# A graph layer on one core: pairs of node tiles, edges by node quarter, operands in PSUM

## The chip, the core and the metric

The kernel runs on one core of one Trainium2 chip. The metric is device time in microseconds (us), lower is better; a kernel's time is the median of several runs. The profile is one execution recorded by the hardware profiler. Engines: PE (TensorE matmul; PEld its weight loads), DVE (VectorE), ACT (ScalarE), POOL (GpSimd), SP (issues plain DMAs). SBUF is the on-chip memory of 128 partitions, PSUM the matmul's output memory of eight banks.

## The reference

One layer over a graph of N = 6250 nodes with D = 256 features and 206,250 edges (`src`, `dst`, sorted by `dst`). Three branches share a normalised input, and a mixture of experts follows:

```python
xn = layernorm(x)
# graph attention, 4 heads of 64
h = xn @ W;  el = h @ Wl.T;  er = h @ Wr.T
e = exp(leaky_relu(el[src] + er[dst], 0.2))
w = e / maximum(segment_sum(e, src), 1e-12)[src]
gnn = elu(stack([segment_sum(w[:, k:k+1] * h[dst], src) for k in range(4)], 1) + b)
# linear attention over all nodes (q softmax over features, k over nodes), rms norms
mix = rmsnorm(linear_attention(rmsnorm(xn)) @ w_out + b_out) + xn
x = x + gnn.reshape(N, 256) + mix
# eight experts of 256 hidden units, each node takes the best two
t = layernorm(x)
out = x + t + sum_e combine[:, e] * (gelu(t @ w1[e] + b1[e]) @ w2[e] + b2[e])
```

So every edge needs the row `h[dst]` with `er[dst]`, and its weighted sum lands at `src`. The edges come sorted by `dst`, so the kernel sorts them by `src` itself.

## The kernel before

Nodes are in 49 tiles of 128 (NT), edges in 1612 columns of 128 (EC, one edge per partition). The work has three parts.

**Sort and projection** (to about 632 us). The loop at the end of the first part calls `project` for 13 groups of four node tiles (layer norm statistics on DVE, transposes and one projection matmul on PE, q, k, v and the rows of the gather table `table`, 64 features and 4 values er), and `sort_batch` for 51 batches of BW = 32 edge columns, three after each group. `sort_batch` builds a one-hot `ob` of each edge's tile number `src >> 7` (50 columns; L320), counts per column (`n_ps` L326), scans them (L330), takes off the count itself (`before` L335), and finds by matmuls (`r_ps` L349, L350) each edge's rank among the batch's edges of its tile. Rank and a one-hot of ranks `ohp` (L372) place the edge's two f16 numbers (`rv` L368, parts of `dst` and of the place in the tile) by matmul into `g_ps` (L377), copied to `grid`: for each tile, each batch and each rank one edge. `context` then computes the attention's 128 x 128 context (key maximum `kmax` L293, `kv` L414). After that the block at L476 to L515 scans the counts of all batches and writes `to_p` and `to_c`, the partition and column at which every edge of a tile will stand.

**Edges** (from 645.5 us on). For each node tile b:

- `pack(b)`: one-hots of column (`ohc` L785) and partition (`ohp` L799) of each edge; `rc` (L791) is `ohc` times the edge's numbers; 51 matmuls into `s_ps` (L804) give the tile's 35 columns of edges (CPT) densely. From it come the row numbers `dst_x` (L813) and the place of the source within the tile, `loc` (L819).
- `gather(dst_x)` (L824, L830): 35 indirect DMAs, one per column, each bringing 128 rows of 68 floats into a seventh of `xe` (pieces of EB = 7 columns, 12 buffers). POOL issues them.
- `sources(b, k, ...)`, five times per tile, called one tile ahead by `look`: `oh` (L842, one-hot of `loc`, 7 x 128), seven transposes `t_ps` (L850), a copy to SBUF `ohT` (L852, ACT), seven matmuls with `elp` into `e_ps` (L854): el of each edge's source.
- `weights`: sum of three parts (L862), five additions of the gathered er (L867), leaky ReLU (L868), exp to `ew` (L870).
- `sums`, five times: the one-hot cast to f32 `oh32` (L875, ACT), `v` = row x weight for the four heads (L879, DVE, two operands in SBUF), seven matmuls `a_ps` (L887) that add 260 columns at the source's place in the tile.
- `heads` divides by the sum of the weights into `x2`.

**Attention and experts** run in pieces between these. `some_more()` is called once after each `sums`, so five times per tile, and performs the next piece of the generators in `todo`: first the 39 pieces of `attention()`, then, appended after each group of four tiles, `finish_steps`: `front` (elu, second layer norm, transposes `tokT` L648, router logits L653), `route` (top two; a matmul for `b2`, L704), eight `expert(e)` (`h_ps` L714, gelu `hT` L722 on ACT, `y_ps` L726, `x` L730 on DVE) and `store`. `h_ps` and `y_ps` have two PSUM buffers each. Groups are of four tiles, the last of one.

The framework's scheduler orders the instructions of each engine from this program and puts the waits in. POOL's queue holds, during the edge part, nothing but the gathers, in order of `pack`. The order of calls around the gathers is:

```python
for k in range(nk):                       # nk = 5
    sums(k, ohs[k], xes[k], ew, a_ps)
    if b + 1 < NT:
        look(b + 1, k)
    if k == 1 and b + 2 < NT:
        dst_x, loc = pack(b + 2)
        ready[b + 2] = (gather(dst_x), loc)
    some_more()
```

A second program follows under `tc.If(over_n > 0)`: if a tile has too many edges for its columns (`flag`), the sums are computed column by column.

Of the kernel before, what the change touches and what calls it, by code (L numbers as in the profile page):

```python
# [8 lines left out]
F32 = mybir.dt.float32  # L9
# [8 lines left out]
P = 128  # L18
GT = 4
BW = 32  # L20
# [3 lines left out]
EB = 7  # L24
# [3 lines left out]
def tile_gps_layer(  # L28
# [40 lines left out]
    NBT = -(-EC // BW)  # L69
    NB = NT + NT % 2  # L70
    BB = 512 // NB
    BB = 8 if BB > 8 else BB
    assert BW % BB == 0 and CPT % EB == 0
    TW = FO + H
    VW = HF + H
    PW = 3 * HID + TW + H
    KW = 2 * HID + 1
    O_TAB = 3 * HID
    O_EL = O_TAB + TW
    assert NPAD > N and PW <= 512 and last > 0  # L80

    groups = [(t0, min(GT, NT - t0)) for t0 in range(0, NT, GT)]

# [9 lines left out]
    nc.vector.tensor_copy(iota_f, iota_i)  # L93
    iota_h = cp.tile([P, P], F16, name="iota_h")
    nc.vector.tensor_copy(iota_h, iota_i)
    iota_b = cp.tile([P, P], BF16, name="iota_b")
    nc.vector.tensor_copy(iota_b, iota_i)
# [11 lines left out]
    elp = cp.tile([P, NT, 3, H], BF16, name="elp")  # L109
# [3 lines left out]
    grid = cp.tile([P, NT, NBT, 2, 2], F16, name="grid")  # L113
# [39 lines left out]
    def load_edges(pool):  # L153
        return load_ids(pool, "src_i", src, NT * P), load_ids(pool, "dst_i", dst, N)
# [19 lines left out]
    tri = sp.tile([P, P], F16, name="tri")  # L174
    nc.vector.tensor_scalar(tri, iota_f, piota, None, op0=OP.is_gt)
    ones16 = sp.tile([P, P], F16, name="ones16")
    nc.vector.memset(ones16, 1.0)
    delta = sp.tile([NB, NB], F16, name="delta")
    nc.vector.tensor_scalar(delta, iota_f[:NB, :NB], piota[:NB], None, op0=OP.is_equal)
    ntot = cp.tile([NT, NBT], F32, name="ntot")  # L180
# [5 lines left out]
    with tc.tile_pool(name="ids", bufs=1) as lp:  # L186
# [4 lines left out]
        def twice(a):  # L191
            return a[:, :, None].to_broadcast([P, EC, 2])

        nc.vector.tensor_single_scalar(t_i, src_i, 7, op=OP.logical_shift_right)
        nc.vector.tensor_copy(bid, twice(t_i))
        nc.vector.tensor_single_scalar(t_i2, dst_i, 3, op=OP.logical_shift_right)
        nc.gpsimd.tensor_copy(va, twice(t_i2))
        nc.vector.tensor_scalar(
            dst_i, dst_i, 7, 8, op0=OP.bitwise_and, op1=OP.logical_shift_left
        )  # L200
        nc.vector.tensor_single_scalar(src_i, src_i, P - 1, op=OP.bitwise_and)
        nc.vector.scalar_tensor_tensor(t_i, src_i, 1.0, dst_i, op0=OP.add, op1=OP.add)
# [5 lines left out]
        out=wcat[:, :, O_TAB:O_TAB + FO], in_=gnn_W.rearrange("(c p) f -> p c f", p=P)  # L208
# [21 lines left out]
    for c in range(DC):  # L230
        wt_ps = mps.tile([FO, P], F32, name="tp")
        nc.tensor.transpose(wt_ps, wcat[:, c, O_TAB:O_TAB + FO], ident)
# [4 lines left out]
        nc.scalar.copy(wcat[:, c, O_TAB + FO:PW], wlr_ps)  # L237
# [9 lines left out]
    def project(t0, n):  # L247
# [16 lines left out]
        tab = qw.tile([P, GT, TW], F32, name="tab")  # L264
        for j in range(n):
            t = t0 + j
            xn = qw.tile([P, D], F32, name="xn")
            nc.vector.tensor_scalar(
                xn, xt[:, j, :], stats[:, t, 0:1], rstd[:, t:t + 1],
                op0=OP.subtract, op1=OP.mult,  # L270
# [15 lines left out]
            nc.scalar.copy(tab[:, j, :], pr[:, O_TAB:O_EL])  # L286
            nc.vector.tensor_copy(el[:, t, :], pr[:, O_EL:PW])
            rows = P if t < NT - 1 else last
            k_t = kv[:rows, t, :HID]
            if t == 0:  # L290
                nc.vector.tensor_copy(kmax, k_t)
            else:
                nc.vector.tensor_max(kmax[:rows], kmax[:rows], k_t)  # L293
        nc.sync.dma_start(
            out=table[t0 * P:(t0 + n) * P, :].rearrange("(t p) f -> p t f", p=P),
            in_=tab[:, :n, :],
# [9 lines left out]
    def sort_batch(t):  # L306
        c0 = t * BW
        w = min(BW, EC - c0)
        cs = slice(c0, c0 + w)

# [13 lines left out]
        n_ps = sps.tile([NB, BW], F32, name="n_ps")  # L324
        for c in range(w):
            nc.tensor.matmul(  # L326
                n_ps[:, c:c + 1], lhsT=ob[:, c, :], rhs=ones16[:, 0:1], start=True, stop=True
            )
        inc = sw.tile([NB, BW], F32, name="inc")
        nc.vector.tensor_tensor_scan(  # L330
            inc[:, :w], ones[:NB, 0:1].to_broadcast([NB, w]), n_ps[:, :w], 0.0,
            op0=OP.mult, op1=OP.add,
        )
        before = sw.tile([NB, BW, 2], F16, name="before")
        nc.vector.tensor_tensor(  # L335
            before[:, :w], inc[:, :w, None].to_broadcast([NB, w, 2]),
            n_ps[:, :w, None].to_broadcast([NB, w, 2]), op=OP.subtract,
        )
        nc.scalar.copy(ntot[:, t:t + 1], inc[:NT, w - 1:w])
        ahead = sw.tile([NB, BW, NB], F16, name="ahead", bufs=1)  # L340
        nc.vector.tensor_tensor(
            pairs(ahead[:, :w]), two(before[:, :w], NB // 2), row(delta, NB // 2), op=OP.mult
# [3 lines left out]
        for i, a in enumerate(range(0, w, BB)):  # L346
            z = min(w, a + BB)
            part = r_ps[:, i, :(z - a) * NB]
            nc.tensor.matmul(part, lhsT=tri, rhs=flat(ob[:, a:z]), start=True, stop=False)  # L349
            nc.tensor.matmul(  # L350
                part, lhsT=ones16[:NB, :], rhs=flat(ahead[:, a:z]), start=False, stop=True
            )
        nf = w // BB
        nc.scalar.copy(
            r16[:, :nf * BB, :].rearrange("p (i c) b -> p i (c b)", c=BB),
            r_ps[:, :nf, :BB * NB],
        )
# [3 lines left out]
        rank = sw.tile([P, BW], F16, name="rank")  # L361
        with nc.allow_low_precision("one summand of each sum is not zero"):
            nc.vector.tensor_reduce(rank[:, :w], r16[:, :w], axis=AX.X, op=OP.add)
        rank2 = sw.tile([P, BW, 2], F16, name="rank2")
        nc.vector.tensor_copy(rank2[:, :w], rank[:, :w, None].to_broadcast([P, w, 2]))
# [9 lines left out]
        g_ps = sps.tile([P, 2 * NB], F32, name="g_ps")  # L375
        for c in range(w):
            nc.tensor.matmul(  # L377
                g_ps, lhsT=ohp[:, c, :], rhs=flat(rv[:, c]), start=(c == 0), stop=(c == w - 1)
            )
# [675 lines left out]
```

## Time and profile before

| | us |
|---|---|
| median of 9 runs | 4252.88 (4215.78 to 4276.84) |
| profiled execution | 4219.04, of which the span is 4217.3 |
| first gather starts | 645.5 |
| last gather starts | 4075.1 |
| gathers | 1715, 947 ns the median of one, 1962.5 in all |
| `a_ps` L887 matmuls on PE | 938.3 in all (3430 passes) |
| `v` L879 on DVE | 493.1 in all (245) |
| `ohp` L799 of 2048 elements on DVE | 177.6 in all (147) |
| POOL idle until `loc` L819 comes | 1463.0 in 20 waits, 624.3 of them the first |

A row of the profile's group list gives an instruction's line, engine, operation, the names of what it writes and reads, shapes and count; then the busy time of all, the mean duration of one, and the idle time just before them with what ended it. "remote" is an end that the profile can put down to no instruction of its list; "issue" is time in which the engine waited for nothing that the profile shows. A matmul in f32 runs in two passes, so L887 counts 3430 for 1715 matmuls. PEclk is the clock that PE was granted, as a share of full speed. In windows, the numbers after a span are busy microseconds of each engine with the count of instructions.

### The profile page before, as it was taken

The page shows a single profiled execution, that of the slowest core. Times are in us where ns is not written, and L with a number is a line of the kernel's source. Part 1 is how long each engine was busy: PE and PEld are TensorE (multiplying, and loading weights), DVE is VectorE, ACT ScalarE, POOL GpSimd, SP SyncE. Part 2 cuts the span into 40 slices and gives each one's busy share as a digit, 9 for nine tenths or more (in the row PEclk, how much of TensorE's full clock was granted, in tenths as well). Part 3 has the DMA queues.
Part 4 walks back from the last instruction along what each step waited for, and adds up shares of the span by engine and source line. Part 5 has one row for each costly group of instructions (what it writes and reads, how often), then busy time and mean ns, then how long its engine had stood idle before and what let it go on. Part 6 is the DMA issues. An engine that isn't in the chain of part 4 may idle for free.

```text
span 4217.3 us, 42641 instructions
## 1 busy us (share of the span) xinstructions
PE 2557.0 (61%) x16398; PEld 1805.8 (43%) x16398; DVE 2078.4 (49%) x3763; ACT 1053.2 (25%) x1888; POOL 1969.3 (47%) x1726
## 2 busy tenths in 40 slices
PE   6888772464467776547457276186275376562758
PEld 3444541343354544425335155154254254452546
DVE  8888993464573443524435145145135245352443
ACT  2323221242332231222222022022122223121223
POOL 0000006676774364643735725725636447557330
PEclk9777765776788877768678688587587688775879
DMA  1000101122131010100101101101101001111010
GB/s 53 19 19 16 9 1 33 40 49 47 40 84 22 13 31 15 29 17 17 29 12 21 31 10 21 32 10 23 25 12 29 17 17 29 18 22 29 12 18 7
DMA packets 106661, 103.22 MB, mean 24 GB/s; under 512 B 42694, under 2 KB 78756, under 8 KB 106452
## 3 DMA queue, kind: packets, MB, share of 16 engines
q0 software_dynamic: 54880, 59.82, 8.3%
q1 hardware_dynamic: 49876, 39.73, 3.1%
q8 instruction: 131, 2.15, 0.2%
q10 hardware_dynamic: 1696, 0.89, 0.1%
q14 instruction: 78, 0.64, 0.1%
HBM read 85.69 MB, written 14.63 MB: 24 GB/s over the span
## 4 chain that ended last, share of the span: by engine, by line
PE 25%; another core or an unknown queue 19%; issue 10%; POOL 9%; DVE 4%; ACT 2%; DMA 1%; DVEq 0%; ACTq 0%; POOLq 0%
POOL xe L830 9%; PE y_ps L726 8%; PE a_ps L887 8%; PE h_ps L714 7%; DVE v L879 2%; PE t_ps L850 1%; PE y_ps L704 1%; ACT ohT L852 1%; DMA xe<-table,dst_x 1%; PE y_ps L653 1%; DVE rc L791 0%; ACT hT L722 0%; DVE ohp L799 0%; PE s_ps L804 0%
## 5 line engine op out<-in xcount | busy, mean ns | idle before, releaser
L830 POOL DMA_INDIRECT xe<-table,dst_x x1715 | 1962.5, 1144 | 2092.4 <-DVE loc L819 1463.0
L887 PE MATMUL a_ps<-v,oh 128*128 128x260 f32 x3430 | 938.3, 425 | 133.3 <-DVE v L879 97.0
L887 PEld LDWEIGHTS a_ps<-v,oh 128*128 128x128 f32 x3430 | 714.8, 214 | 268.3 <-issue 117.3
L879 DVE TENSOR_TENSOR v<-xe,ew 128x1792 f32<-128x1792 f32 x245 | 493.1, 2020 | 523.4 <-remote 285.0
L726 PE MATMUL y_ps<-w2s,hT 128*128 128x256 f32 x1568 | 436.1, 422 | 304.2 <-issue 158.7
L875 ACT CAST oh<-oh 128x896 f32<-128x896 bf16 x245 | 230.0, 939 | 1252.5 <-PE a_ps L887 782.9
L730 DVE SCALAR_TENSOR_TENSOR x<-y_ps,comb,x 128x256 f32<-128x256 f32 x392 | 183.7, 482 | 644.2 <-remote 379.1
L726 PEld LDWEIGHTS y_ps<-w2s,hT 128*128 128x128 f32 x1568 | 307.9, 207 | 433.6 <-issue 213.9
L714 PE MATMUL h_ps<-tokT,w1s 128*128 128x512 f32 (+1 forms) x832 | 392.2, 594 | 2.7 <-ACT hT L722 2.7
L852 ACT COPY ohT<-t_ps 128x896 bf16<-128x896 bf16 x245 | 220.8, 901 | 438.4 <-remote 302.0
L854 PE MATMUL e_ps<-elp,ohT 128*128 128x12 bf16 x1715 | 82.1, 171 | 319.1 <-ACT ohT L852 178.1
L804 PE MATMUL s_ps<-rc,ohp 128*128 128x72 f16 x2499 | 122.8, 210 | 216.6 <-issue 163.0
L854 PEld LDWEIGHTS <-ohT 128*128 128x128 bf16 x1715 | 68.9, 99 | 379.7 <-ACT ohT L852 222.4
L722 ACT ACTIVATE hT<-h_ps,b1s 128x512 f32<-128x512 f32 (+1 forms) x208 | 135.4, 662 | 331.1 <-PE h_ps L714 175.3
L804 PEld LDWEIGHTS <-ohp 128*128 128x128 f16 x2499 | 109.2, 108 | 235.8 <-issue 176.8
L799 DVE TENSOR_TENSOR ohp<-to_p,iota_h 128x2048 f16<-128x2048 f16 x196 | 193.5, 1000 | 28.7 <-remote 17.7
L653 PE MATMUL y_ps<-rwT,tokT 128*128 128x8 f32 x196 | 34.9, 287 | 253.7 <-ACT tokT L649 138.8
L714 PEld LDWEIGHTS h_ps<-tokT,w1s 128*128 128x128 f32 x832 | 145.5, 196 | 98.0 <-issue 91.7
L867 DVE TENSOR_TENSOR z<-z,xe 128x28 f32<-128x28 f32 x245 | 44.0, 186 | 253.6 <-DMA xe<-table,dst_x 214.0
L842 DVE TENSOR_TENSOR oh<-iota_b,loc 128x896 bf16<-128x896 bf16 x245 | 147.9, 617 | 41.1 <-issue 25.4
L377 PE MATMUL g_ps<-rv,ohp 128*128 128x100 f16 x1612 | 111.9, 245 | 82.7 <-DVE ohp L372 82.7
L850 PE MATMUL t_ps<-identb,oh 128*128 128x128 bf16 x1715 | 159.4, 237 | 4.1 <-ACT ohT L852 3.8
(229 smaller groups left out, 2801.5 us busy)
## 6 DMA issues: line engine op xcount, KB each, us to landing
xe<-table,dst_x POOLq DMA_INDIRECT x1715
xt<-in_x_dram SPq DMA_DIRECT2D x24, 512.0 KB
base_y<-xt SPq DMA_DIRECT2D x12, 512.0 KB
yt<-base_y SPq DMA_DIRECT2D x12, 512.0 KB
out_dram<-x SPq DMA_DIRECT2D x12, 512.0 KB
w1s<-in_L_ffn_w_dram SPq DMA_DIRECT2D x8, 256.0 KB
w2s<-in_L_ffn_w_dram SPq DMA_DIRECT2D x8, 256.0 KB
table<-tab SPq DMA_DIRECT2D x12, 136.0 KB
```

The lines of the kernel that those rows point to most:

```text
L714: nc.tensor.matmul(h_ps[:, :w], lhsT=w1s[:, e, c, f * P:(f + 1) * P], rhs=tokT[:, c, :w], start=(c == 0), stop=(c == DC - 1),)
L726: nc.tensor.matmul(y_ps, lhsT=hT[:, f, j * P:(j + 1) * P], rhs=w2s[:, e, f, :], start=(f == 0), stop=(f == FC - 1),)
L730: nc.vector.scalar_tensor_tensor(x2[:, j, :], y_ps, comb[:, j, e:e + 1], x2[:, j, :], op0=OP.mult, op1=OP.add,)
L799: nc.vector.tensor_tensor(pairs(ohp[:, :m]), twos(to_p[:, b, t0:t0 + m], P // 2), iota_2.to_broadcast([P, m, P // 2, 2]), op=OP.is_equal,)
L804: nc.tensor.matmul(flat(s_ps), lhsT=ohp[:, t - t0, :], rhs=flat(rc[:, t]), start=(t == 0), stop=(t == NBT - 1),)
L830: nc.gpsimd.indirect_dma_start(out=xe[:, j, :], out_offset=None, in_=table, in_offset=bass.IndirectOffsetOnAxis(ap=dst_x[:, c:c + 1], axis=0),
L850: nc.tensor.transpose(t_ps[:, j, :], oh[:, j, :], identb)
L852: nc.scalar.copy(ohT, t_ps)
L854: nc.tensor.matmul(e_ps[:, k * EB + j, :], lhsT=ohT[:, j, :], rhs=elp[:, b].rearrange("p i h -> p (i h)"), start=True, stop=True,)
L875: nc.scalar.copy(oh32, oh)
L879: nc.vector.tensor_tensor(v[:, :, :HF].rearrange("p j (h f) -> p j h f", h=H), xe[:, :, None, :FO].to_broadcast([P, EB, H, FO]), e_k[:, :, ...
L887: nc.tensor.matmul(a_ps, lhsT=oh32[:, j, :], rhs=v[:, j, :], start=(c == 0), stop=(c == CPT - 1),)
```

## The change

1. **Pairs of tiles.** The sort's key is `src >> 8`: 25 pairs (NQ), so 26 columns (NB) in place of 50. Ranks and `grid` are per block of CB = 16 edge columns (101 blocks NBT), two blocks to a batch of 32. The count matmul has two columns (one, none), so one scan with resets gives the exclusive counts, negated, and `before` goes; the lower triangle `tri` becomes `upto`. The reduce works on a folded half; the doubled rank is copied by ACT.
2. **Projection.** The normalised input `xn` is computed by ACT, `el` is copied by POOL from the projected rows, the key maximum is one reduce at the end, `kv - krow` is done by POOL. A table row has 69 floats: er, the 64 features, a one.
3. **Placing moves into `pack(q)`,** which now runs per pair, 25 times: one-hots of the edge's node quarter, two matmuls and a scan for each tile of the pair, folds, and the place `to` for the 101 blocks. Then as before `ohc`, `rc`, `ohp`, `s_ps`, with 72 columns instead of 36, in seven chunks of 16 blocks. Two times 35 gathers are issued at once. A tile's edges are in order of the quarter (S = 4, SN = 32 nodes) of their source; with fixed windows of columns, a column can hold edges of one or two neighbouring quarters, 45 cells of column and quarter in all (CELLS).
4. **Operands in PSUM.** One bank holds `ew_s` (a copy of `ew`), the bias `gb_s`, the iotas `iota_p` (f16) and `iota_q` (bf16) and `edges`, the pair's numbers, copied in by `pack`. `hps` drops from two buffers to one.
5. **`look`** (in place of `sources`): one `oh` of 12 x 4 x 32 bf16, 12 transposes, two copies `ohT`, one matmul that clears `e_ps` and 12 with 48 columns (`elw`: for each quarter its own rows of el, zero elsewhere).
6. **`sums`**, four times per tile: `ohw` = one-hot x weight (f32, 10 to 12 columns x 4 heads x 32 nodes), and a matmul for each cell with the gathered rows as weights (65 columns, the ones give the sum of weights) and 128 columns of `ohw`. `v` and the cast of `oh` go. The result is transposed: a copy `a_s` and four transposes bring it back to nodes by features.
7. **Buffers.** `xe` is a whole tile of 35 columns, three buffers; the gathered er is added in one operation, kept in the program's order.
8. **Order.** `pack(q + 1)` is called in the pair's first tile at k = 1. `some_more()` is called four times per tile. `expert` is split into `hidden` and `result`: the first layer of expert e alternates with the second of e - 1. Groups for the experts are 11 of four tiles, then 3, 1 and 1.
9. The overflow flag is computed at the end, from counts kept by `pack`.

The core of the diff:

```diff
-        nc.vector.tensor_single_scalar(t_i, src_i, 7, op=OP.logical_shift_right)
+        nc.vector.tensor_single_scalar(t_i, src_i, 8, op=OP.logical_shift_right)
...
+    def pack(q):
...
+        for u in range(U):
+            ohs = gw.tile([P, S, NBT], F16, name="ohs")
+            nc.vector.tensor_tensor(
+                ohs, uh[:, None, :].to_broadcast([P, S, NBT]), quarter[:, u], op=OP.is_equal
+            )
+            here = pl.tile([P, S, NBT], F32, name="s_ps")
+            nc.tensor.matmul(flat(here), lhsT=upto, rhs=flat(ohs), start=True, stop=True)
+            total = pt.tile([P, S, NBT], F32, name="t_ps")
+            nc.tensor.matmul(flat(total), lhsT=ones16, rhs=flat(ohs), start=True, stop=True)
+            nc.vector.tensor_tensor_scan(
+                flat(inc[:, u]), ones[:, 0:1].to_broadcast([P, S * NBT]), flat(total),
+                float(u * CW * P), op0=OP.mult, op1=OP.add,
+            )
...
+        nc.vector.tensor_copy(
+            edges, grid[:, q].rearrange("p t i two -> p (t i two)").bitcast(F32)
+        )
...
+            ohc = gw.tile([P, PB, U * CW], F16, name="ohc")
+            nc.vector.tensor_tensor(
+                pairs(ohc[:, :m]), twos(to[:, 0, t0:t0 + m], U * CW // 2),
+                iota_2[:, :, :U * CW // 2].to_broadcast([P, m, U * CW // 2, 2]),
+                op=OP.is_equal,
+            )
...
+            ready[q * U + u] = (gather(dst_x[:, u * CW:u * CW + CPT]), loc)
...
-        for k in range(CPT // EB):
-            xe = gw.tile([P, EB, TW], F32, name="xe", bufs=12)
+        xe = gw.tile([P, CPT, TW], F32, name="xe", bufs=3)
+        for c in range(CPT):
+            nc.gpsimd.indirect_dma_start(
...
+        tc.keep_in_program_order(nc.vector.tensor_add(z, z, xe[:, :, :H]))
...
+        nc.vector.tensor_copy(ew_s, ew)
...
+    def sums(i, oh, xe, a_ps):
+        g0, g1 = CELLS[i]
...
+        nc.vector.tensor_tensor(
+            ohw[:, :n],
+            oh[:, g0:g1, i, None, :].to_broadcast([P, n, H, SN]),
+            ew_s[:, c0:c0 + n, :, None].to_broadcast([P, n, H, SN]),
+            op=OP.mult,
+        )
+        for c in range(c0, c0 + n):
+            nc.tensor.matmul(
+                a_ps[:, i].rearrange("f h n -> f (h n)"),
+                lhsT=xe[:, c, H:],
+                rhs=ohw[:, c - c0].rearrange("p h n -> p (h n)"),
+                start=(c == c0), stop=(c == c0 + n - 1),
+            )
...
+                if k == 1 and b % U == 0 and b + U < NT:
+                    pack(b // U + 1)
```

## The prediction

> **What bounds the kernel now.** I read the busy shares and the chain first, then windows stage by stage, then waits and the timeline of one period. The page's rows:
>
> ```profile
> span 4217.3 us, 42641 instructions
> PE 2557.0 (61%) x16398; PEld 1805.8 (43%) x16398; DVE 2078.4 (49%) x3763; ACT 1053.2 (25%) x1888; POOL 1969.3 (47%) x1726
> PE 25%; another core or an unknown queue 19%; issue 10%; POOL 9%; DVE 4%; ACT 2%; DMA 1%; DVEq 0%; ACTq 0%; POOLq 0%
> ```
>
> No engine is busy for more than 61%, and the chain has 19% that it can give to nobody: the stages must be taken apart. Windows (span, then busy time of PE, PEld, DVE, ACT, POOL, PEclk, DMA) of the sort, 0 to 632 us:
>
> ```profile
> 0.00:358.00 358.00, 273.31 (x2263) 151.67 (x2264) 305.85 (x560) 107.70 (x297) 6.86 (x11) 0.80 0.10 29
> 358.00:632.00 274.00, 207.64 (x1801) 128.13 (x1800) 248.22 (x376) 79.89 (x179) 0.00 (x0) 0.71 0.06 7
> ```
>
> DVE works 554 of 632 us (88%) and PE 481 (76%): the sort is bound by DVE, PE close behind. POOL has nothing to do; its first gather starts at 645.5 us. From there the kernel is one loop of 49 node tiles. From 1702.7 to 3473.0 us 24 tiles take 1770.3 us, 73.8 us each, and four tiles make a period: 105 gathers, a pause, 35 gathers, a pause. One period, and the 35 gathers of it cut in two:
>
> ```profile
> 1999.10:2150.90 151.80, 52.78 (x401) 42.81 (x400) 50.42 (x80) 25.00 (x38) 120.04 (x105) 0.65 0.15 28
> 2150.90:2216.60 65.70, 59.61 (x302) 40.77 (x303) 38.10 (x84) 23.79 (x38) 0.01 (x1) 0.90 0.01 1
> 2216.60:2263.80 47.20, 27.55 (x115) 18.55 (x114) 11.13 (x18) 6.45 (x9) 36.84 (x35) 0.81 0.13 25
> 2263.80:2290.40 26.60, 24.86 (x180) 19.41 (x179) 17.18 (x30) 10.12 (x16) 0.03 (x1) 0.95 0.10 22
> ```
>
> ```profile
> 2216.60:2237.60 21.00, 20.33 (x100) 13.97 (x98) 10.16 (x16) 5.77 (x8) 17.02 (x14) 1.00 0.12 23
> 2237.60:2263.80 26.20, 7.22 (x17) 4.58 (x16) 0.97 (x2) 0.69 (x1) 19.81 (x21) 0.66 0.14 27
> ```
>
> While no gather runs, PE is busy 84.5 of 92.3 us (over all six periods 0.90); while gathers run, 80.3 of 199. A burst begins well (PE 97% of 21 us), then everything but POOL nearly stops (PE 28%, in three like windows 15 to 34%, mean of the four 0.24). The timeline shows the stop:
>
> ```profile
> 1791.95 0.94 ACT L875 CAST oh<-oh 128x896 f32<-128x896 bf16 x1 [18.22 <-remote]
> 1792.02 2.03 DVE L879 TENSOR_TENSOR v<-xe,ew 128x1792 f32<-128x1792 f32 x1 [17.74 <-remote]
> 1792.30 2.57 POOL L830 DMA_INDIRECT xe<-table,dst_x  x1 [0.30 <-DMA xe<-table,dst_x]
> ...
> 1795.17 0.95 POOL L830 DMA_INDIRECT xe<-table,dst_x  x1 [0.30 <-issue]
> ...
> 1860.74 0.37 ACT L649 COPY tokT<-y_ps 128x256 f32<-128x256 f32 x1 [34.08 <-remote]
> ```
>
> ACT and DVE wait 18 and 34 us for something from PE, which is idle too; the last wait ends 6 us after the burst's last gather. So hand-offs from PE come late while gathers follow one another cleanly. Why, the trace doesn't tell. The loop is bound by gather time plus PE work that doesn't fit beside it. Third line: a gather that meets a v (L879) takes 2.57 us in place of 0.95; 152 of 1715 do, 248.7 us more in all. A clean gather is 0.95 us plus 0.30 of issue, 1.25 us, 43.75 us per tile.
>
> **The sort.** Buckets fall from 50 to 26 columns. Prices from the same operations at two sizes: f16 tensor_tensor 966 ns at 1600, 2281 at 4096 elements, so 123 + 0.527 per element, 0.56 us at 832; the reduce 1800 ns at 1600 and 768 at 600, so 0.61 us at 448. Per batch: five operations (ob, ahead, r, two rv) 5 x (0.97 - 0.56) = -2.03; reduce -1.19, fold +0.34 (384 elements); `before` -0.20; rank copy -0.18; a scan twice as long at most +0.2, taken +0.1. Sum -3.16, x 51 = -161 us. In project and context: xn -19.5 (to ACT, busy 188 of the 632 us), running kmax -13.4, its one reduce of 6144 elements +6.3, kv minus krow -8.3 (to idle POOL, ahead of its first gather), el copies -8 (same queue), shift 13 x 0.2 = +2.6: -40. DVE 554 to 353 us. PE: rank matmuls halve, -83 of 166.4 us (L349, L350), 481 to 398; PE is the bound now. At the share that the binding engine has today (0.88) 398 / 0.88 = 453 us. The placing stage goes (13 us after 632 stay for pack, in which DVE is busy 13.3); pack of a pair has 34,744 elements x 0.59 = 20.5 us and some 25 small ones at 0.2 to 0.5, 30 to 37 us. First gather at 490, not 645.5: **-155** us. Bounds: PE at 0.80, 398 / 0.80 + 35 = 533 (-112); DVE at 0.88, 353 / 0.88 + 35 = 438 (-207).
>
> **PE in the loop, per tile.** Before: 164.8 / 4 = 41.2 us. a_ps now 70 passes x 0.274 = 19.1; then 45 matmuls of two passes with 128 columns: 90 x 0.159 (h_ps 128x128, 10.2 us by 64) = 14.3, or 90 x 0.208 (its weight loads today) = 18.7; taken 16, -3.1. Transposes 35 to 12, -2.1; e_ps 35 to 13, -0.9; s_ps 50 of 144 columns at 0.075 (g_ps of 100: 0.069), +1.3; here and total 2 x 0.42 (r_ps rows of 400), +0.8; four head transposes 4 x 0.26 (L648), +1.0. Sum 38.2 us.
>
> **DVE and ACT in the loop.** v (5 x 2.02 = 10.1 us) goes; ohw has 5760 elements, 6.5 us at v's 1.13 ns. Pack: 12,036 elements to 17,372 per tile, +3.2; scans, folds, copies of pack +4 (some 20 operations per pair, 0.2 to 0.5 us); one oh of 1536 for five of 896, -2.2; the five z additions become one, -0.7; the rest +3. 29.2 to 33 us, under PE. ACT loses the oh32 cast (4.7 us) and half of ohT (2.5): it waits 782.9 us for a_ps today, so that earns nothing by itself.
>
> These DVE prices hold if an operand in PSUM costs nothing. No row has a 16-bit tensor_tensor with one. Lower bound 0.59 ns per element (L799, 1217 ns by 2048), upper 1.13 (v, f32): 18,900 x 0.54 = +10.2 us per tile. I take the lower: operand width is what the rows differ by. Trainium skill, "VectorE: DVE Perf Modes", "The perf-mode tier table": a tensor_tensor with any operand in PSUM runs at 1x, half the 16-bit rate; the section "Why PSUM operands drop a tier" bars only a mode that tensor_tensor never has. By the table DVE has 10.2 us more per tile, and the sum would be 4288 in place of 3785 if all of that set the end.
>
> What the move buys shows in the 2.57 us row: with ew_s, iotas and edges in PSUM, a large DVE operation has one SBUF input, and gathers should all take 1.25 us. Against the gain: the 41.8 us after 1702.7, full of v and ohp, have PE at 81% beside slow gathers, while the clean stretch after it has 17%. Cleaner gathers may also mean a longer stop.
>
> **The order of gathers.** Pack now runs once per pair and issues 70 gathers in a row. In the program's DVE order the first tile's z addition comes only 27 to 46 instructions after dst_x and waits for the whole tile (43.75 us); behind it on DVE are the next ohw and the expert sums, which PE waits for. Today this wait is 214 us in 31 times (L867). Whatever is late there is the first tile of a pair; its second is hidden beside the first's work. So per pair: 87.5 us of gathers; in it PE does 0.97 x 21 = 20.4 us, then 66.5 us at 0.20 (between 0.24 above and 0.17 in the long clean stretch) = 13.3; the other 76.4 - 33.7 = 42.7 us at 0.90 take 47.5 us. 135 us per pair, 67.5 per tile, 6.3 less than 73.8. For 40 tiles 252 us; the first nine, beside attention (59 us per tile today, 332 gathers in 560 us), get half, 28. **-280**, bounds 0 (the stop begins after 10 us: 9.7 + 77.5 x 0.17 = 22.9, rest 59.5, 147 per pair) and -530 (0.35 in the stop, 124 per pair, counted in the same way).
>
> **The tail.** After the last gather 141 us pass, PE busy 119. The last blocks are 3, 1 and 1 tiles in place of 4 and 1, so a block less is left, but one-tile experts load the same weights: **-30**, bounds -60 and +10.
>
> **Sum.** Profiled execution: 4219.0 (span 4217.3 and 1.7 around it) - 155 - 280 - 30 = 3754. The median of the runs shown, 4252.88, is 1.008 times that; so the median after is 3754 x 1.008 = 3785 us. Timed runs spread by 0.7% either way; about 0.5% is what a comparison can tell from none.
>
> **Rivals**, as medians.
> 1. *Only the sort earns.* Clean bursts of 70 stop PE as long as the two bounds above say: (4219 - 155 - 30) x 1.008 = 4066. For it the 17% stretch; against it fewer and larger hand-offs (12 transposes, two ohT copies). Chance 0.20.
> 2. *The stop goes away.* If it comes from the number of PE's hand-offs, which falls by a quarter, POOL and PE run side by side: 43.75 us of gathers per tile, PE 38.2 / 0.90 = 42.4 beside them, some 5 for the pause at each pack: 490 + 49 x 49 + 110 = 3001, or 3025. For it: the first 21 us of a burst. Against: stops of 35-gather bursts with 17 instructions in them. Chance 0.13; half-way cases lie between.
> 3. *Slower: DVE with operands in PSUM.* Place: ohc, rc, ohp of pack and oh; price 10.2 us per tile. Pack stands ahead of each pair's gathers, POOL waits for it, and DVE at 43 us passes PE's 38. If all of it is on the path, 49 x 10.2 = +500: 3754 + 500 = 4254, or 4288 (+0.8%). It decides from (4219 - 3754) / 49 = 9.5 us per tile, 0.50 ns per element, on. Against it: DVE has 42% idle in the loop. Chance 0.14.
> 4. *The change doesn't do what it says*: a quarter overflows its cells and the slow path runs. That is a loop of 1612 columns, far above all this; 0.01.
>
> **The numbers.** Forecast 3785, chance 0.52, its own range 3600 to 3980 (front and loop half-way to their bounds). Range 3390 to 4250: it leaves out most of rival 2 and the upper part of 3. Faster 0.82 (forecast, 2, and 0.17 of rival 1), within 0.5% 0.04 (0.03 of 1, 0.01 of 3), slower 0.14 (0.13 of 3, and 4).
>
> **What would show it.** First gather at 440 to 530 us. ohp of 2048 elements near 1.2 us (right) or 2.3 (rival 3). Gathers at 0.95 us nearly all, none of 2.6. 70-gather bursts with PE above 0.9 in the first 20 us and about 0.2 later. About 135 us per pair. Wrong if pairs take 147 or under 110, or if the binding engine in the sort is idle for over 20%.

## The result and the profile after

The changed kernel takes 4704.26 us (median of 20 runs, 4688.76 to 4712.37) beside 4237.91 us for the kernel before: ratio 1.113, 95% interval 1.1108 to 1.1151 (the two medians alone give 1.110). Forecast were 3785 us, range 3390 to 4250. One thing must be known to read the rest: the runs fall into groups in which the kernel before takes 4208 to 4238 us (the first, with this result), 3348 to 3352 us (the second), 4071 us (the third) and 3349 us (the last run), and every ratio below is against the kernel before in the same group. The record gives the chips of these groups the numbers 1, 11, 2 and again 1, so it doesn't tell whether what differs is the chip or something that changed on it.

The profiled execution after has a span of 4690.6 us, 473.3 more than before. Three marks cut it:

| part | before | after | difference | predicted |
|---|---|---|---|---|
| start to first gather | 645.5 | 455.1 | -190.4 | -155 |
| first to last gather's end | 3430.6 | 4100.7 | +670.1 | -280 |
| last gather's end to the end | 141.2 | 134.8 | -6.4 | -30 |

The page after, its span, busy times and chain:

```profile
span 4690.6 us, 39432 instructions
PE 2329.6 (50%) x15347; PEld 1675.7 (36%) x15347; DVE 1967.9 (42%) x4111; ACT 715.2 (15%) x1467; POOL 1674.8 (36%) x1779
another core or an unknown queue 41%; PE 23%; DVE 19%; issue 6%; ACT 2%; POOL 1%; DMA 0%; DVEq 0%; ACTq 0%; SPq 0%
```

Every engine has less work than before, and the share of the chain that belongs to nobody has gone from 19% to 41%. Windows after (span, busy time of PE, PEld, DVE, ACT, POOL, PEclk, DMA): the sort in two pieces, then one pair of tiles, its 70 gathers and the pause after them, and the next burst cut in two:

```profile
0.00:300.00 300.00, 238.58 (x2688) 137.64 (x2689) 258.47 (x537) 145.58 (x456) 24.71 (x49) 0.82 0.14 40
300.00:440.00 140.00, 92.70 (x1216) 64.99 (x1216) 128.87 (x229) 44.72 (x124) 23.84 (x15) 0.60 0.11 2
...
2118.10:2205.30 87.20, 23.39 (x102) 16.03 (x99) 9.49 (x15) 1.96 (x3) 66.14 (x70) 0.59 0.15 28
2205.30:2294.80 89.50, 68.19 (x401) 52.46 (x402) 51.93 (x100) 15.56 (x22) 0.05 (x1) 0.81 0.03 7
2294.80:2309.30 14.50, 12.79 (x126) 11.80 (x124) 14.06 (x25) 4.82 (x6) 11.42 (x11) 1.00 0.25 61
2309.30:2383.50 74.20, 5.70 (x25) 4.85 (x24) 1.96 (x5) 0.74 (x2) 56.22 (x60) 0.53 0.16 28
```

This pair takes 177 us; later ones alternate between about 161 and 177, 85 us per tile on the mean, where four tiles took 295 and one 73.8. In the burst that is cut in two PE falls from 88% to 8% after 14.5 us and stays there for 74 us. That burst is a sharp one: over the 24 bursts of 70 gathers PE is busy for 62% of the first 14.5 us and 14% of the rest, 19.1 us of work per burst. The gathers themselves and the largest group beside them, with the waits (engine and line waiting, for what, us in all, times, longest):

```profile
L927 POOL DMA_INDIRECT xe<-table,dst_x x1715 | 1626.3, 948 | 2574.3 <-PE a_ps L996 1740.1
...
L989 DVE TENSOR_TENSOR ohw<-oh,bank 128x1280 f32<-128x1280 bf16 x196 | 323.0, 1648 | 1058.5 <-remote 847.6
```

```profile
DVE ohw L989 <- remote: 847.6, 28, 57.3
ACT ohT L956 <- remote: 817.4, 12, 95.0
```

The mean of a gather is 948 ns where it was 1144, and 1697 of 1715 are under 1 us (1389 before): the change did to the gathers what it says. DVE and ACT wait for PE up to 95 us, against 56 before. The timeline of the burst that begins at 2294.8 us:

```profile
2308.54 0.82 PE L996 MATMUL a_ps<-ohw,xe 128*65 128x128 f32 x6
...
2333.02 0.37 ACT L675 COPY tokT<-y_ps 128x256 f32<-128x256 f32 x1 [27.70 <-remote]
...
2334.78 1.49 PE L996 MATMUL a_ps<-ohw,xe 128*65 128x128 f32 x6
2360.38 0.17 DVE L683 COPY lg<-y_ps 128x8 f32<-128x8 f32 x1 [26.73 <-remote]
```

PE does a piece in a few microseconds and then 24 us pass before ACT or DVE sees it. A hand-off is the semaphore update with which PE tells that a piece is done. Counted over the trace's semaphore records, each put to the PE instruction that ended last before it, PE's hand-offs came late by 5964 us in sum while gathers ran (643 hand-offs, the latest by 75 us) and by 80 us while none ran; before it was 1565 and 83 us. These sums are estimates: the trace has 2609 update records for PE's 2726 hand-offs, and nearly all that are missing belong to gather time. The recorded hand-offs of DVE and ACT in the same time are late by 0.6 us at most, so it is PE's that are held.

### The profile page after: what moved, and what is told of

Same layout as the page of the kernel before. It is cut to its first block, busy times and chain, and to the rows that moved or that the text cites. A ratio compares the mean times of both kernels' runs of the same rounds, so it can differ in the third digit from the quotient of the medians.

```text
span 4690.6 us, 39432 instructions
## 1 busy us (share of the span) xinstructions
PE 2329.6 (50%) x15347; PEld 1675.7 (36%) x15347; DVE 1967.9 (42%) x4111; ACT 715.2 (15%) x1467; POOL 1674.8 (36%) x1779
## 4 chain that ended last, share of the span: by engine, by line
another core or an unknown queue 41%; PE 23%; DVE 19%; issue 6%; ACT 2%; POOL 1%; DMA 0%; DVEq 0%; ACTq 0%; SPq 0%
PE a_ps L996 8%; PE h_ps L739 5%; PE y_ps L755 5%; DVE rc L889 4%; DVE ohp L894 4%; DVE ohc L882 2%; DVE ohw L989 2%; DVE inc L853 1%; PE y_ps L679 1%; DVE x L759 1%; POOL xe L927 1%; PE y_ps L730 1%; PE y_ps L567 1%; ACT ohT L956 0%
## 5 line engine op out<-in xcount | busy, mean ns | idle before, releaser
L927 POOL DMA_INDIRECT xe<-table,dst_x x1715 | 1626.3, 948 | 2574.3 <-PE a_ps L996 1740.1
L996 PE MATMUL a_ps<-ohw,xe 128*65 128x128 f32 x4410 | 671.4, 308 | 475.1 <-issue 433.9
L996 PEld LDWEIGHTS a_ps<-ohw,xe 128*65 128x65 f32 x4410 | 591.7, 160 | 535.0 <-issue 480.8
L989 DVE TENSOR_TENSOR ohw<-oh,bank 128x1280 f32<-128x1280 bf16 x196 | 323.0, 1648 | 1058.5 <-remote 847.6
L739 PE MATMUL h_ps<-tokT,w1s 128*128 128x512 f32 (+2 forms) x896 | 425.2, 596 | 87.0 <-ACT hT L747 69.9
L899 PE MATMUL s_ps<-rc,ohp 128*128 128x144 f16 x2525 | 263.6, 279 | 189.6 <-DVE ohp L894 189.6
L899 PEld LDWEIGHTS <-ohp 128*128 128x128 f16 x2525 | 227.6, 123 | 259.9 <-DVE ohp L894 249.6
L747 ACT ACTIVATE hT<-h_ps,b1s 128x512 f32<-128x512 f32 (+2 forms) x224 | 142.1, 634 | 1112.5 <-PE h_ps L739 365.7
L889 DVE TENSOR_TENSOR rc<-ohc,bank 128x1152 f16<-128x1152 f16 (+1 forms) x350 | 226.5, 686 | 1.4
L894 DVE TENSOR_TENSOR ohp<-to,bank 128x2048 f16<-128x2048 f16 (+1 forms) x175 | 193.6, 1106 | 0.0
L567 PE MATMUL y_ps<-cw,qT 128*128 128x256 f32 x98 | 47.5, 576 | 266.6 <-ACT qT L565 162.0
```

The source lines that it names most:

```text
L567: nc.tensor.matmul(o_ps, lhsT=qT, rhs=cw, start=True, stop=True)
L739: nc.tensor.matmul(h_ps[:, :w], lhsT=w1s[:, e, c, f * P:(f + 1) * P], rhs=held["tokT"][:, c, :w], start=(c == 0), stop=(c == DC - 1),)
L747: nc.scalar.activation(held[e][:, f, :w], h_ps[:, :w], AF.Gelu, bias=b1s[:, k:k + 1])
L889: nc.vector.tensor_tensor(pairs(rc[:, :m, i, :]), pairs(ohc[:, :m]), twos(edges_q[:, t0:t0 + m, i, :], U * CW // 2), op=OP.mult,)
L894: nc.vector.tensor_tensor(pairs(ohp[:, :m]), twos(to[:, 1, t0:t0 + m], P // 2), iota_2.to_broadcast([P, m, P // 2, 2]), op=OP.is_equal,)
L899: nc.tensor.matmul(flat(s_ps), lhsT=ohp[:, t - t0, :], rhs=flat(rc[:, t - t0]), start=(t == 0), stop=(t == NBT - 1),)
```

## The experiments

Each is an edit of the changed kernel unless said otherwise.

**First group (kernel before 4208 to 4236 us).**

The operands back in SBUF:

```diff
-    bank = pv.tile([P, 512], F32, name="bank")
+    bank = gw.tile([P, 512], F32, name="bank", bufs=1)
```

> The changed kernel with the bank of operands (weights, bias, iotas, the pair's edge numbers) in SBUF instead of PSUM, nothing else. Theory A (PE's hand-offs are held while gathers follow one another at 1.25 us without a break; whatever lengthens the pitch lets them through): each ohw and oh has two SBUF inputs again and lengthens gathers it meets to 2 to 3 us, so PE is busy for 0.30 or more of the gather time instead of 0.22 and the time falls to 4350 to 4600. Rival B (large DVE operations are slower with an operand in PSUM): ohc, rc, ohp, ohw get shorter in the records and pack ends sooner; 4400 to 4600 with the gathers still at 0.95 us. Rival C (what stops PE is the length of a burst of 70, or the wait for the whole tile): 4690 to 4750.

4272.7 us, ratio 1.012 (0.9955 to 1.0281): 432 us less than the changed kernel. The windows of a burst and the `ohp` rows of both kernels, this one first:

```profile
2243.60:2334.70 91.10, 27.94 (x156) 20.89 (x154) 15.49 (x28) 5.72 (x7) 70.06 (x70) 0.67 0.16 33
```

```profile
L893 DVE TENSOR_TENSOR ohp<-to,bank 128x2048 f16<-128x2048 f16 x150 | 182.7, 1218 | 41.5 <-PE s_ps L898 30.8 <-remote 10.7
```

```profile
L894 DVE TENSOR_TENSOR ohp<-to,bank 128x2048 f16<-128x2048 f16 x150 | 181.6, 1211 | 0.0
```

DVE's operations cost the same with an operand in PSUM (1211 ns) as in SBUF (1218): rival B falls. 87 gathers are over 1.5 us, against 2, and the lateness falls from 5964 to 4093 us. That is Theory A's direction, but the scheduler also put DVE's work into another order (36 instructions between `dst_x` and the first z addition of its pair on the mean, those of pack left out, 26 in the changed kernel), so one run doesn't settle how much is whose.

A break after each gather:

```diff
-            nc.gpsimd.indirect_dma_start(
+            tc.keep_in_program_order(nc.gpsimd.indirect_dma_start(
...
+            if c % 1 == 1 - 1:
+                rest_t = gw.tile([P, 448], F32, name="rest_t", bufs=1)
+                tc.keep_in_program_order(nc.gpsimd.memset(rest_t, 0.0))
```

The gathers, too, are kept in the program's order here and in all runs with a break. That alone is not what helps: e5_pace192 below has it as well.

> The changed kernel with a POOL memset of 448 floats (about 0.46 us by the rate of the other memsets) after every gather; the output is the same. Theory A: the pitch goes from 1.25 to about 1.75 us, 70 gathers take 122 us instead of 87, but PE's hand-offs flow and PE is busy for over 0.5 of that time: a pair takes 120 to 150 us instead of 174, in all 3500 to 4100. Rival C (burst length, whole-tile wait) and a bound by POOL: 35 us more per pair, 5300 to 5550.

3686.4 us, ratio 0.873 (0.8596 to 0.8864), 1018 us less than the changed kernel, by giving POOL 842 us more to do. The groups, and one burst:

```profile
L927 POOL DMA_INDIRECT xe<-table,dst_x x1715 | 1658.6, 967 | 719.8 <-PE a_ps L999 325.3 <-issue 279.1 <-ACT q_all L554 100.0
...
L935 POOL MEMSET rest_t<- 128x448 f32 x1715 | 842.1, 491 | 1.3
```

```profile
2236.70:2349.20 112.50, 48.24 (x318) 34.80 (x316) 43.96 (x94) 17.40 (x25) 101.09 (x140) 0.68 0.13 27
```

Pitch 1.60 us, PE at 43% in this burst and 62% in the gather time between 1500 and 3300 us, and not one of the 1598 hand-offs of gather time that have a record is late by 0.2 us (some 470 have none). Rival C, that the burst's length or the wait for the whole tile stops PE, asked for 5300 or more; it falls.

The same POOL time in other portions, and a shorter break (against e2_pace):

```diff
+            if c % 7 == 6:
+                rest_t = gw.tile([P, 896], F32, name="rest_t", bufs=1)
+                for _ in range(4):
+                    tc.keep_in_program_order(nc.gpsimd.memset(rest_t, 0.0))
```

> As the paced kernel, with the same POOL time in other portions: seven gathers at the 1.25 us pitch, then four memsets of 896 floats (about 3.2 us). Theory A with a backlog that forms after 8 to 12 clean gathers: the pauses come before it forms, and hand-offs wait for 3 to 10 us at most; 3500 to 4200, near the paced kernel. If only the pitch of single gathers counts, and not the mean rate, it stays at 4600 or more; rival C: 5200 or more.

```diff
-            rest_t = gw.tile([P, 448], F32, name="rest_t", bufs=1)
+            rest_t = gw.tile([P, 192], F32, name="rest_t", bufs=1)
```

> The paced kernel with a memset of 192 floats in place of 448 after every gather: pitch about 1.36 us (0.95 + 0.17 + 0.24) in place of 1.60, against 1.25 without. If hand-offs already flow at this pitch, POOL's 70 gathers take 95 us in place of 112 and a pair falls from 130 to about 115: 3300 to 3500. If the pitch must be well over 1.25 us, the stops come back in part: 3900 to 4500. Rival (only the memset's length counts as POOL time): 3686 - 49 x 35 x 0.24 = 3270.

Pauses of 3.4 us after every seven gathers give 3811.4 us (ratio 0.903, 0.8888 to 0.9164), lateness 534 us, none over 5 us: pauses before the stop forms do nearly as well. A memset of 192 floats (pitch 1.39 us) gives 4341.37 us (1.032, 1.0055 to 1.0579) with 3411 us of lateness. So between a pitch of 1.39 and 1.60 us the stops go.

The kernel before with the break of 448 floats after every gather:

```diff
+                rest_t = gw.tile([P, 448], F32, name="rest_t", bufs=1)
+                tc.keep_in_program_order(nc.gpsimd.memset(rest_t, 0.0))
             xes.append(xe)
```

> The kernel before, with a POOL memset of 448 floats after every gather, nothing else. Theory A: the stops of its bursts of 105 and 35 go too; POOL needs 35 x 1.75 = 61 us per tile and more where v meets a gather, PE 41: the tile takes 62 to 68 us instead of 73.8, in all 3700 to 4000. Without Theory A (gather time is simply added to): 49 x 16 x 0.5 or more is added, 4500 to 4900.

3899.69 us, ratio 0.9235 (0.9094 to 0.9376). The stop was already there before the change, and costs that kernel at least 337 us; lateness 20 us in place of 1565.

Bursts of 35 (`xe` with two buffers), and the break with the bank in SBUF:

```diff
-        xe = gw.tile([P, CPT, TW], F32, name="xe", bufs=3)
+        xe = gw.tile([P, CPT, TW], F32, name="xe", bufs=2)
```

> The changed kernel with two buffers of a tile's gathered rows in place of three, so that the second tile's 35 gathers wait until the first buffer in use is free: bursts of 35 in place of 70. If the stop needs a run of clean gathers to begin, each burst has its first 12 to 15 us free and PE does some 12 us more per pair: 4350 to 4600. If the loss is in proportion to the gathers whatever their grouping, 4690 or, with the gathers now exposed to the tile that waits for them, up to 5000.

```diff
-    bank = pv.tile([P, 512], F32, name="bank")
+    bank = gw.tile([P, 512], F32, name="bank", bufs=1)
...
+            rest_t = gw.tile([P, 448], F32, name="rest_t", bufs=1)
+            tc.keep_in_program_order(nc.gpsimd.memset(rest_t, 0.0))
```

> The paced kernel (448 floats) with the bank of operands in SBUF. Theory A: once hand-offs flow, longer gathers only cost POOL: 3700 to 3800, 0.1 us per gather more than the paced kernel or 15 to 110 us in all; so the operands in PSUM are a small gain here and the loss of 430 us only without pacing. If operands in PSUM are bad in themselves (DVE), it falls below 3600.

4424.33 us (1.0514, 1.0414 to 1.0615): 280 us less than with bursts of 70. PE is busy for 34% of the gather time in place of 22%, as is to be expected when twice as many bursts each have their better beginning. And 3610.26 us (0.858, 0.8485 to 0.8674), the best in this group, under the expected 3700 to 3800. That miss matters: no recorded hand-off is late in either of the two paced kernels, so the 76 us are not the stop. In this one POOL issues in long unbroken runs (805 gathers in a row to 3505 us), in the other it pauses 6 to 20 us at most packs. The order on DVE differs again (62 instructions between `dst_x` and the z addition, 34 in the other); that it is the reason was not tested.

No indirect DMA at all, the same bytes by plain DMAs from SP:

```diff
-            nc.gpsimd.indirect_dma_start(
...
+            nc.sync.dma_start(out=xe[:, c, :], in_=table[c * P:(c + 1) * P, :])
```

> The changed kernel with each gather replaced by a plain DMA from SP's queue that brings 128 neighbouring rows of the table (column c takes block c), the same bytes into the same places; the rows are not the edges' rows, so the sums are others. POOL then issues nothing. If the stop comes from POOL's issuing of indirect DMAs, PE's hand-offs flow: PE is bound, 455 + 49 x 44 / 0.9 + 110 = 2960, in all 2900 to 3400. If it comes from the DMA traffic into SBUF (the same bytes), 4000 or more.

2563.1 us (0.609), below the range expected. As many of the table's bytes, brought into the same tiles, stop nothing, and no hand-off is late:

```profile
PE 2084.6 (81%) x15347; PEld 1551.4 (61%) x15347; DVE 1959.0 (77%) x4111; ACT 697.2 (27%) x1454; POOL 48.5 (2%) x64
```

The changed kernel's 1715 gathers occupy 2141 us, and it takes 2141 us longer than this one. That the two agree to the microsecond is partly chance, since PE did some work in each burst; but little was hidden beside the gathers.

**Second group (kernel before 3348 to 3352 us).**

One group of operands at a time in SBUF:

```diff
-    ew_s = bank[:, :CPT * H].rearrange("p (c h) -> p c h", h=H)
+    ew_s = gw.tile([P, CPT, H], F32, name="ew_s", bufs=1)
```

> The changed kernel with only the edge weights ew_s in SBUF; iotas, edge numbers and bias stay in PSUM. ohw is the DVE operation that runs while gathers run. Theory A: most of the 431 us that the whole bank in SBUF gave back comes back with this alone, 4330 to 4500, with gathers that meet an ohw at 2 us or more. If it was the changed order on DVE in that run and not the meeting of ohw and gathers: 4600 to 4720.

```diff
-    iota_p = bank[:, words:words + P // 2]
+    iota_p = gw.tile([P, P // 2], F32, name="iota_p", bufs=1)
...
-    edges = bank[:, words:words + 2 * NBT]
+    edges = gw.tile([P, 2 * NBT], F32, name="edges", bufs=1)
```

> The changed kernel with the operands of pack alone (iota_p and the pair's edge numbers) in SBUF; ew_s and iota_q stay in PSUM. Pack runs while no gather does, since it makes their addresses: Theory A expects little, 4600 to 4720. If the order on DVE or pack's operations are the cause, most of the 431 us comes back here: 4270 to 4450.

3350.21 us (ratio 0.9996, 0.9983 to 1.0008) and 3417.89 us (1.0199, 1.0172 to 1.0227). Neither theory could be told: the kernel before took 3352 us here, and no hand-off is late by 0.2 us in gather time in any profile of this group, though gathers follow one another at 1.25 us. No update record is missing either (2727 for 2726 hand-offs in the changed kernel, e13_after below). So the stop is not a property of the program alone.

Shorter breaks, with the bank in SBUF (against e7_pace_sbuf):

```diff
-            rest_t = gw.tile([P, 448], F32, name="rest_t", bufs=1)
+            rest_t = gw.tile([P, 320], F32, name="rest_t", bufs=1)
```

(256 in the second run.)

> The paced kernel with its bank in SBUF and a memset of 320 floats in place of 448. POOL issues without a break in that kernel (1.76 us per gather), so it is bound by POOL: 0.11 us less per gather is 190 us: 3420 to 3480 if hand-offs still flow at a mean pitch of 1.65 us. If they begin to wait: 3600 to 4000.

> The same with 256 floats: pitch 1.43 us where nothing meets a gather, about 1.58 in the mean. If hand-offs flow at 1.43 us: 3320 to 3400. In the kernel paced by 192 floats (pitch 1.36 to 1.39, bank in PSUM) they did not, so the threshold lies between 1.39 and 1.60 us; beyond it the time rises to 3700 to 4200.

3507.11 us (1.0462, 1.044 to 1.0484) and 3410.41 us (1.0181, 1.0164 to 1.0199): without a stop a break only costs POOL time, 97 us for 64 floats per gather. Where the threshold lies between 1.39 and 1.60 us can't be read here.

The changed kernel and the kernel before, both unaltered, and `ew_s` in SBUF once more (the diff of e9_ew):

> The changed kernel itself, unaltered, beside the kernel before. In the last group of runs the kernel before took 3352 us, 21% less than in the others, and no hand-off of PE came late in the four profiles of that group although gathers followed one another at 1.25 us. If this group is like it: the change is then judged without the stop: by the terms of the prediction (sort -190 as measured, less PE work in the loop, a_ps and transposes) 3150 to 3350; by the two kernels that differ from it in one operand each (3350 and 3418) 3350 to 3420, so that the loop gives back what the sort earns. If this group is like the earlier ones: 4690 to 4720 beside 4185 to 4290.

> The kernel before, for its profile beside the changed one on the same chip. Where the kernel takes 3350 us: no late hand-offs (sum of their lags under 20 us against 1565), PE busy for 0.6 or more of the gather time against 0.40, first gather at 645 us as before, and a period of four tiles near 225 us against 295. Otherwise as recorded: 4185 to 4290.

> Once more the changed kernel with only ew_s in SBUF. Where hand-offs are held: Theory A 4330 to 4500, against 4600 to 4720 if it was the order on DVE. Where they aren't: 3350 again, 0 to 60 us under the changed kernel.

The changed kernel takes 3473.99 us (1.0377, 1.0356 to 1.0398), the kernel before as a run of its own 3351.11 us, and the one with `ew_s` in SBUF 3347.97 us (0.9998, 0.9988 to 1.0008). Even without any stop the change loses 126 us, against the expected 3150 to 3420. With `ew_s` in SBUF it loses nothing, although its bursts take longer (2301 us against 2156); its breaks between bursts are 468 us against 737. DVE's order differs there (34 instructions against 26), which may be the reason and was not tested. The chain of the kernel before in this group, and its gathers:

```profile
POOL 50%; issue 14%; PE 10%; DMA 4%; DVE 3%; ACT 1%; POOLq 0%; DVEq 0%; ACTq 0%
```

```profile
L830 POOL DMA_INDIRECT xe<-table,dst_x x1715 | 2054.8, 1198 | 1154.6 <-DVE loc L819 632.5 <-issue 504.4 <-DMA xe<-table,dst_x 15.5
```

It is bound by POOL: 632.5 us idle before the first gathers, then one stream to the end, 1.50 us per gather. The changed kernel in the same group, one burst and the pause after it, and DVE's wait:

```profile
2268.80:2356.30 87.50, 74.70 (x414) 55.69 (x413) 39.40 (x75) 18.20 (x28) 66.43 (x70) 0.92 0.15 29
2356.30:2379.40 23.10, 15.26 (x126) 13.02 (x124) 23.10 (x46) 0.32 (x1) 0.00 (x1) 0.70 0.11 26
```

```profile
DVE z L977 <- DMA xe<-table,dst_x: 854.8, 39, 30.9
```

PE is busy for 85% of this burst, 44% of the next and 57% of all gather time. But then POOL stands still for 23 us while DVE, busy for all of it, makes the next pair's addresses. DVE had waited 855 us at the z additions, with that pack behind them. Time in bursts fell from 2577 us (1.503 per gather) to 2156 (1.257), and the breaks between bursts rose from 9 to 737 us (loops of 2585.5 and 2893.0 us): +307, less 192.6 saved in the sort, plus 5.0 in the tail, is the 119.8 us between the two profiles.

**Third group (kernel before 4071 us), in which PE is stopped as in the first.**

`pack` one tile earlier (the first two pairs before the loop), and the same with the diff of e9_ew:

```diff
-                if k == 1 and b % U == 0 and b + U < NT:
-                    pack(b // U + 1)
+                if k == 1 and b % U == 1 and b + 1 + U < NT:
+                    pack(b // U + 2)
```

> The changed kernel with pack called one tile earlier (in the odd tile before, for the pair after the next; the first two before the loop), nothing else: on DVE some 100 instructions in place of 24 then lie between dst_x and the z addition that waits for the whole tile. Theory D (without the stop, the change loses because pack comes late and DVE waits at z for the tile, 855 us in 39 waits, with the next pack behind it): where the kernel before takes 3350 us, the waits fall under 300 us, gathers run nearly without a break and the time goes from 3474 to 3050 to 3250, under the kernel before. Rival E (operands in PSUM or one h_ps buffer are what costs): 3430 to 3500. Where the kernel before takes 4240 us: the stop begins earlier in the work but is as long; 4500 to 4720.

> The same early pack with ew_s in SBUF as well. Theory D: where the kernel before takes 3350 us, within 40 us of the kernel with early pack alone, since the 126 us that ew_s in SBUF gave without it came from the order on DVE that it changed (27 instructions in place of 24 on the mean, over 35 in many pairs) and longer gathers cost a little: 3050 to 3280. Rival E: 126 us under it. Where the kernel before takes 4240 us: below it, since gathers meet ohw again, 4250 to 4450.

4343.94 us (1.0685, 1.0605 to 1.0765), under the expected 4500, and 3934.88 us (0.9674, 0.9558 to 0.979), under the expected 4250. Side by side in one group, the one operand that meets the gathers makes 409 us. Lateness is 5272 and 3781 us, the pitch 1.25 and 1.34 us per gather, and PE is busy for 34% and 47% of the gather time between 1500 and 3300 us, as Theory A has it. `pack` is early in both (100 and 83 instructions on DVE between `dst_x` and z), and DVE waits at z for gathered rows for 0 and 22.5 us in all, so that wait doesn't make the difference. How much of the 409 us is the stop stays open all the same: without a stop, and with pack late, the same edit gave 126 us. Whether early pack alone turns the loss of the second group (Theory D) was not run there.

**All three together, in a last run (kernel before 3349 us).**

The diffs of e16_early and e9_ew, and

```diff
+            rest_t = gw.tile([P, 320], F32, name="rest_t", bufs=1)
+            tc.keep_in_program_order(nc.gpsimd.memset(rest_t, 0.0))
```

> All three findings together: ew_s in SBUF, pack one tile earlier, and a memset of 320 floats (pitch 1.48 us where nothing meets a gather) after every gather. Where the kernel before takes 4050 to 4250 us: Theory A says that hand-offs flow at this pitch or nearly so, POOL needs 70 x 1.6 = 112 us per pair and never waits for pack: 455 + 24.5 x 112 + 130 = 3330, in all 3250 to 3500, a ratio of 0.77 to 0.85; if 1.48 us is under the threshold, 3600 to 3900. Where it takes 3350 us: bound by POOL as well, 3250 to 3400.

3315.53 us, ratio 0.9903 (0.9885 to 0.9921): 1% below the kernel before beside it, and below the 3474 us that the changed kernel takes in the second group, with 1715 gathers at 1.59 us in two unbroken runs and no late hand-off. It was not run where PE is stopped, so whether its pitch (median 1.50 us) is slow enough stays open.

## Why the prediction was wrong, point by point

**The step that failed** is "in it PE does 0.97 x 21 = 20.4 us, then 66.5 us at 0.20". That makes 33.7 us of PE's work per burst; PE did 19.1 (mean of the 24 bursts of 70): 10.8 us in the first 21 us, a share of 0.52, and 8.3 in the rest, a share of 0.12. In the burst cut in two above, the free beginning lasted 14.5 us and the rest ran at 0.08. I took the 21 us from bursts whose first gathers were slowed (14 in 21 us), while the change takes the slowing away: after 11 gathers the stop is there. I had the warning row, 81% beside slow gathers and 17% after, in these two windows of the kernel before:

```profile
1702.70:1744.50 41.80, 33.72 (x323) 28.56 (x322) 34.38 (x50) 18.09 (x26) 35.40 (x22) 0.92 0.09 18
1744.50:1854.50 110.00, 18.31 (x77) 13.89 (x77) 15.97 (x30) 6.84 (x12) 84.69 (x84) 0.55 0.17 31
```

I wrote "Cleaner gathers may also mean a longer stop", but bounded the loss at 0 in place of pricing it; that bound, rival 1, was 670 us off. e2_pace beside e5_pace192, e3_pause, e8_sp and the lateness of the pair e16_early and e18_ew_early show the cause in the first and the third group: there, indirect gathers that follow one another undisturbed hold PE's hand-offs. The operations that I counted as a cost to POOL let PE's work through.

The stop is not all of the 670 us. Where nothing is stopped, the loop already grows by 307 us (2585.5 to 2893.0). Against that group the loop before takes 845 us longer in the first group and the changed loop 1208. If the stop is all that sets the two groups apart, it costs the changed loop 363 us more than it cost the loop before.

**The pause for pack** is the other part, and a step of its own that failed. "42.7 us at 0.90 take 47.5 us": the stretch without gathers took 89.5 us in the pair shown and 82 on the mean of all pairs, PE at 0.76 and 0.72. More work was left over, and pack, on DVE, lies in that stretch. In the second group, where nothing is stopped, such breaks alone are 737 us of POOL's time. I named late pack and the z wait behind it (28 us in all in the first group, 855 in the second), but let PE's work fill the time; the order lets POOL and DVE take turns. With it fall rival 2's 49 us per tile: without a stop it is 59 (2893 / 49), and 52.8 in the kernel before.

**PE's work.** Predicted 76.4 us per pair, from 82.4 before. In the second group PE is busy for 1196 us between 1500 and 3300 us, in which 1069 gathers run, 78.3 us per 70; in the kernel before for 1311 us beside 1161 gathers, 79.1. So the size was nearly right, and of the saving of 6 us hardly 1 is there: the 82.4 us were read where PE is stopped, and the same kernels' busy time is longer there.

**The sort**: -190.4 for -155, within its bounds. The direction was right, the bound was not: DVE, not PE, still binds (387 of 440 us, 88%, where 353 were predicted; PE 331 us, 75%, where 398 were).

**Operands in PSUM on DVE** (rival 3): right to take the lower bound, `ohp` 1211 ns for 1217. The table that I quoted from the Trainium skill, "VectorE: DVE Perf Modes", "The perf-mode tier table", gives tensor_tensor with any PSUM operand the 1x rate; here f16 operations with one operand in PSUM keep the 16-bit rate, and the measurement decides.

**The tail**: -6 for -30, within its bounds. **Rival 1** named the right warning and the wrong end; **rival 4** can be put aside: nothing of a slow path's 1612 steps stands in the trace.

## What to carry to other kernels

When two engines seem to disturb each other, look at what a third does in the same windows before taking the disturbance away: where PE is stopped here, its results got through mainly beside the slow gathers. A bound of zero loss needs a row that shows it, above all when a row in the same profile shows the opposite. And a producer made faster is worth its gain only if its next order is ready: compute addresses a whole stage ahead, and keep a wait for the whole batch from standing in front of them. Here that was run without a stop only together with two other edits (e19_ew_early_pace), so its own share isn't shown.

## What the runs showed of the hardware

While POOL issues indirect DMAs at a pitch of 1.25 us, PE's hand-offs to ACT and DVE come up to 75 us late in the first and the third group of runs (5964 us in sum in one run of the changed kernel); in the first group at 1.39 us 3411 us remain, at 1.60 us none is late. In the second group none is late at 1.25 us either. Plain DMAs of as many bytes into the same tiles don't cause it. What holds the hand-offs, and whether the chip or something else sets the groups apart, these runs don't tell. The traces of the stopped groups lack update records just when indirect gathers run, paced or not; whether the recording itself has a part in the stop was not tested.
